# Cross-attention kernel, one core: the first batch's fifth output chunk copied by ScalarE with its bias, its residual added by an accumulating transfer of GpSimd's queue

## The chip, the core and the metric

The kernel runs on one core of a Trainium2 chip. The time is that of the device for one execution, in microseconds (us). The kernel before was run three times: 497.24, 496.01 and 496.43 us, so its median is 496.43 us. One further execution was recorded by the hardware profiler; its span, from the first to the last instruction of the program, is 494.6 us.

The engines are called as the profile calls them: PE (TensorE, matrix products; PEld is its weight load), DVE (VectorE), ACT (ScalarE), POOL (GpSimd), and SP (SyncE, which issues most transfers). Each engine works through a queue of its own in the order in which the program emits instructions; engines wait for each other through semaphores.

## What is computed

Cross-attention of 2 x 2048 tokens of width 640 (20 heads of 32) over 154 context rows of width 1024. The first 77 rows ("text") and the last 77 ("ip") have weights of their own and a softmax each; both results are added, projected, and the bias and the input itself are added. All in float32. Cut to its core:

```
q    = split(x @ Wq.T)                                  # 20 heads of 32
k, v = split(ctx[:, :77] @ Wk.T), split(ctx[:, :77] @ Wv.T)
ki, vi = split(ctx[:, 77:] @ Wk_ip.T), split(ctx[:, 77:] @ Wv_ip.T)
attend = lambda q, k, v: softmax(q @ k.T / sqrt(32)) @ v
out  = merge(attend(q, k, v) + attend(q, ki, vi))
return out @ Wo.T + bo + x
```

## The kernel before

**Layout.** Tensors lie with the channel on the partitions: 640 channels are 5 chunks of 128, and the 2048 tokens of a batch are 4 blocks of 512. A unit `u` (0 to 19) is one batch, one chunk of 4 heads and one half of the tokens; a pair of units shares a chunk (`q = u // 2`, 0 to 9; 0 to 4 are the first batch).

**Order.** The whole order is written by hand: `SCHEDULE` is a string of 1026 words, and `emit` turns each word into the instructions of one step, in that order. Since every engine has one queue, the place of a word sets its place on the queue of its engine. The words that matter here:

- `R`, `K`, `M`, `S`, `E`, `D`, `I`, `N`, `T` with `s.u` (group of 128-token rows `s` of unit `u`): scores on PE (L242), copy to the tile `pb` on ACT (L254), maxima on DVE (L290, L293), subtraction on POOL (L304), exponential on ACT (L310, or row by row with the bias at L278), sums and reciprocals on DVE (L315, L320), normalisation on POOL (L325), 32 x 32 transposes on DVE (L332). `A.q` multiplies by the values on PE (L341), `CA.q` copies the result to `aT` on ACT (L364, L368).
- `q.u.h` is a query projection on PE (L206), `cq` its copy on ACT (L220).
- The output projection of the first batch: chunks 0 to 3 of the output go through Strassen-like products `m1` to `m7` (L499, L509), whose inputs `G` POOL subtracts (L440), and which DVE adds into the tile `acc` (L524, L530). The fifth chunk (128 of the 640 output channels) has a path of its own, below.
- `V`, `X`, `F`, `Y`, `z`, `yz`: the output projection of the second batch by a fast 5 x 5 scheme, the last stage of the kernel: sums of weights (`V`, L864, L866) and of tokens (`X`, L872) on DVE and POOL, products on PE (L887), and their addition into the output on DVE (L827, L830).
- `LX`, `LQ`, `VS` and others issue transfers from SP's queue.

**The fifth chunk of the first batch**, for each token block `i` = 0 to 3: `SF.i.4` (L468, SP) loads the block's residual, 128 x 512 numbers of `x`, into the only tile `res`; `o.i@n` (L480, PE) makes the product in PSUM bank `n`; `co.i` (`store_last`, L490, DVE) adds product, bias and residual into `res`; `SS.i.4` (L474, SP) stores `res`. After the fourth block `res` is used again, for a block of the second batch (L855). The banks are 0 to 7; `R...@0` uses banks 0 to 3 and `R...@1` banks 4 to 7. `o.0` uses bank 3, `o.1` and `o.2` bank 0, `o.3` bank 7.

**Words around the fourth block.** `... E2.18 T0.18 co.3 A.8@0 N1.18 cm4.2 SS.3.4 SS.2.3 SS.2.1 G5.3 T1.18 ... V.P.0.p ... R1.19@1 CA.8 N2.18 ...`. On ACT, `E2.18` and `CA.8` follow each other; on POOL, `N1.18`, `G5.3`, `V.P.0` and `N2.18`.

Of the kernel before, what the change touches and what calls it, by code (L numbers as in the profile page):

```python
# [20 lines left out]
def kernel(  # L21
# [432 lines left out]
    def part_in(t, s, h):  # L454
        return t.rearrange("p (op s) (h t) -> p s h op t", s=2, h=2)[:, s, h]
# [6 lines left out]
    def in_dram_last(t, b, i):  # L462
        return t[ts(NC - 1, P), ds(b * S + i * TB, TB)]

    def fetch(i, part):

        if part == "last":
            nc.sync.dma_start(out=res, in_=in_dram_last(xT, 0, i))  # L468
        else:
            nc.sync.dma_start(out=part_in(acc, *part), in_=in_dram(xT, 0, i, *part))  # L470
# [17 lines left out]
    def store_last(ps, b, i):  # L488
        t = last_of(b, i)
        nc.vector.scalar_tensor_tensor(t, ps, bo_sb[:, NC - 1 :], t, ALU.add, ALU.add)  # L490
# [94 lines left out]
    for t in range(2):  # L585
# [350 lines left out]
```

## Time and profile before

| | |
|---|---|
| median of three runs (lowest to highest) | 496.43 us (496.01 to 497.24) |
| profiled execution, span | 494.6 us |
| PE busy | 489.1 us, 99% of the span |
| DVE busy | 413.9 us, 84% |
| POOL busy | 370.5 us, 75% |
| ACT busy | 309.5 us, 63% |
| granted clock of PE, mean | 1.000 |
| `co.i` on DVE (L490) | 4 instructions, 2.9 us in all, the first at 228.62 us, the last at 388.88 us |

How to read it: "busy" is the union of an engine's instructions. A row of the timeline gives start, length, engine, line, operation, the tile written and those read, the shape, how many instructions the row holds, and in brackets for how long the engine had been idle before it and what ended that idle time. Times in all views count from the start of the span.

### The profile page before, as it was taken

How to read it: one execution, taken by the hardware profiler on the slowest of the kernel's cores; microseconds unless marked ns; L12 is line 12 of the kernel's file. 1: busy time of each engine (PE TensorE's matmuls, PEld its weight loads, DVE VectorE, ACT ScalarE, POOL GpSimd, SP SyncE). 2: the span in 40 equal slices, each digit the busy share in tenths (PEclk: the TensorE clock that was granted, in tenths of full speed). 3: DMA queues.
4: the chain of work that ended last, by engine and by line, in shares of the span. 5: the costliest groups of instructions: out<-in, count | busy, mean ns of one | idle time of the engine just before them, and what ended most of it. 6: DMA issues, size and time to landing. Idle time of an engine off the chain costs nothing.

```text
span 494.6 us, 10484 instructions
## 1 busy us (share of the span) xinstructions
PE 489.1 (99%) x4116; PEld 287.7 (58%) x4116; DVE 413.9 (84%) x416; ACT 309.5 (63%) x1002; POOL 370.5 (75%) x158
## 2 busy tenths in 40 slices
PE   9999999999999999999999999999999999999997
PEld 5666648558557556456566654754755675444443
DVE  0069989989899989979988896687789898999996
ACT  1275788977687778677899786587889862100000
POOL 0069988988988988879886758475689899798700
PEclk9999999999999999999999999999999999999999
DMA  8992046203241724895540666455550212320125
GB/s 278 350 288 80 17 124 181 67 1 95 62 150 44 247 65 146 270 345 178 161 172 27 215 195 223 134 172 183 184 169 19 90 42 85 129 85 2 42 85 212
DMA packets 67105, 69.38 MB, mean 140 GB/s; under 512 B 5488, under 2 KB 47088, under 8 KB 67056
## 3 DMA queue, kind: packets, MB, share of 16 engines
q1 hardware_dynamic: 66048, 67.54, 43.7%
q10 hardware_dynamic: 1008, 1.18, 0.7%
q8 instruction: 32, 0.52, 0.4%
q14 instruction: 17, 0.14, 0.1%
HBM read 54.94 MB, written 10.49 MB: 132 GB/s over the span
## 4 chain that ended last, share of the span: by engine, by line
PE 96%; DMA 3%; ACTq 0%; ACT 0%; DVE 0%; DVEq 0%; issue 0%
PE bank L206 34%; PE bank L887 12%; PE bank L341 11%; PE bank L242 11%; PE bank L499 10%; PE bank L144 9%; PE bank L480 7%; PE bank L509 3%; DMA aT<-in_L_xattn_Wk_ip_dram 2%; DMA x<-in_x_dram 1%; ACTq L538 0%; ACT pb L254 0%; ACTq L552 0%; DVE acc L830 0%; DVEq L931 0%
## 5 line engine op out<-in xcount | busy, mean ns | idle before, releaser
L325 POOL TENSOR_TENSOR pb<-pb,rden 128x1848 f32<-128x1848 f32 (+1 forms) x60 | 176.0, 2943 | 30.4 <-DVE rden L320 23.6
L304 POOL TENSOR_TENSOR pb<-pb,mx 128x1848 f32<-128x1848 f32 (+1 forms) x39 | 121.6, 3129 | 55.4 <-DVE mx L290 55.3
L206 PE MATMUL bank<-x,wq 128*128 128x512 f32 x280 | 125.4, 598 | 0.1
L332 DVE STREAM_TRANSPOSE pb<-pb 128x1920 f32<-128x1920 f32 (+1 forms) x60 | 115.9, 1938 | 9.1 <-POOL pb L325 8.9
L290 DVE TENSOR_REDUCE mx<-pb 128x24 f32<-128x1848 f32 (+1 forms) x50 | 91.6, 1844 | 32.1 <-ACT pb L254 31.9
L254 ACT COPY pb<-bank 128x462 f32<-128x462 f32 (+1 forms) x200 | 85.3, 542 | 29.3 <-PE bank L242 28.9
L315 DVE TENSOR_REDUCE den<-pb 128x24 f32<-128x1848 f32 (+1 forms) x47 | 88.9, 1895 | 15.6 <-ACT pb L310 12.8
L206 PEld LDWEIGHTS bank<-x,wq 128*128 128x128 f32 x280 | 51.7, 190 | 60.0 <-issue 58.8
L310 ACT ACTIVATE pb<-pb 128x1848 f32<-128x1848 f32 (+1 forms) x39 | 65.6, 1684 | 17.5 <-POOL pb L304 17.4
L278 ACT ACTIVATE pb<-bank,mx 128x77 f32<-128x77 f32 x208 | 60.4, 387 | 6.5 <-DVE mx L293 6.5
L278 ACT ACTIVATE pb<-pb,mx 128x77 f32<-128x77 f32 x184 | 54.1, 356 | 1.9 <-DVE mx L290 1.8
L341 PE MATMUL bank<-pb,v 32*32 32x512 f32 x1600 | 55.2, 597 | 0.0
L206 PE MATMUL bank<-x,aT 128*128 128x512 f32 x116 | 51.8, 596 | 0.0
L242 PEld LDWEIGHTS bank<-kT,qT 32*128 32x128 f32 x1024 | 36.1, 184 | 21.6 <-issue 13.3
L144 PE MATMUL bank<-wo_ct,aT 128*128 128x154 f32 x320 | 46.0, 297 | 0.7 <-DMA aT<-in_L_xattn_Wk_ip_dram 0.4
L144 PEld LDWEIGHTS bank<-wo_ct,aT 128*128 128x128 f32 x320 | 43.0, 188 | 4.7 <-issue 3.0
L242 PE MATMUL bank<-kT,qT 32*128 32x154 f32 x1024 | 45.1, 305 | 0.0
L278 ACT ACTIVATION_READ_ACCUMULATOR pb<-bank,mx 128x1 f32 x168 | 44.0, 266 | 0.0
L341 PEld LDWEIGHTS bank<-pb,v 32*32 32x32 f32 x1600 | 29.0, 103 | 22.7 <-issue 10.1
L480 PE MATMUL bank<-aT,wo_ct 128*128 128x512 f32 x80 | 36.3, 595 | 0.0
L206 PEld LDWEIGHTS bank<-x,aT 128*128 128x128 f32 x116 | 21.4, 190 | 23.7 <-issue 23.5
L220 ACT ACTIVATE qT<-bank 128x512 f32<-128x512 f32 x32 | 19.3, 631 | 23.4 <-PE bank L206 23.4
(83 smaller groups left out, 524.2 us busy)
## 6 DMA issues: line engine op xcount, KB each, us to landing
x<-in_x_dram SPq DMA_DIRECT2D x20, 1280.0 KB, 6.7
out_dram<-acc SPq DMA_DIRECT2D x19, 256.0 KB, 2.9
x<-in_x_dram SPq DMA_DIRECT2D x17, 256.0 KB, 5.9
acc<-in_x_dram SPq DMA_DIRECT2D x16, 256.0 KB, 4.4
out_dram<-x SPq DMA_DIRECT2D x15, 256.0 KB, 2.0
v<-vS SPq DMA_DIRECT2D x160, 20.0 KB, 2.7
aT<-in_L_xattn_Wk_dram SPq DMA_DIRECT2D x5, 512.0 KB, 6.0
aT<-in_L_xattn_Wk_ip_dram SPq DMA_DIRECT2D x5, 512.0 KB, 5.5
```

The source lines that it names most:

```text
L144: nc.tensor.matmul(keys_in(out), loaded[n][:, k, :], cT[:, k, :, t, :], start=(k == 0), stop=(k == NCC - 1))
L206: nc.tensor.matmul(pq, weight_of(q)[:, k, :], xs[place_of(u, h)][:, k, :], start=(k == 0), stop=(k == NC - 1), skip_group_check=loose,)
L242: nc.tensor.matmul(ps[g][:, ts(t, 2 * L)], qTs[(u, h)][g * D : (g + 1) * D, ts(st, P)], kT[g * D : (g + 1) * D, c, b].rearrange("p t l -> ...
L254: nc.scalar.copy(keys_of(u, s)[:, :, g], ps[g][:, : n * 2 * L].rearrange("p (n l) -> p n l", n=n))
L278: nc.scalar.activation(row, row if ps is None else rows_in(ps[g], n)[:, t, x], AF.Exp, bias=maxs[(u, s)][:, *one], accum_out=None if den i ...
L290: nc.vector.tensor_reduce(mx, rows_of(u, s), AX.X, ALU.max, negate=negate)
L304: nc.gpsimd.tensor_tensor(rows_of(u, s), rows_of(u, s), maxs[(u, s)].unsqueeze(3).to_broadcast([P, n, 2, L]), ALU.subtract)
L315: nc.vector.tensor_reduce(den_of(u, s), rows_of(u, s), AX.X, ALU.add)
L325: nc.gpsimd.tensor_tensor(rows_of(u, s), rows_of(u, s), rdens[(u, s)].unsqueeze(3).to_broadcast([P, n, 2, L]), ALU.mult)
L332: nc.vector.transpose(p, p)
L341: nc.tensor.matmul(pa[r][g * D : (g + 1) * D, :], v4s[q % 2][rows, g, k, :], zones[rows, :, g, k, :], start=(k == 0), stop=(k == NK - 1),)
L480: nc.tensor.matmul(ps, wo[:, k, ts(NC - 1, P)], rows_of_attention(b, k)[:, i], start=(k == 0), stop=(k == NC - 1),)
```

## The change

`co.i` moves from DVE to ACT: one activation (identity with the bias) copies the product from PSUM to `res`. The load of the residual, `SF.i.4`, is left out. A new word, `AX.i`, takes its place: a transfer issued from GpSimd's queue which reads the residual from memory and adds it into `res` (`accum_op=ALU.add`). `SS.i.4` stores `res` as before; it now follows `AX.i`.

```diff
     def fetch(i, part):
-        if part == "last":
-            nc.sync.dma_start(out=res, in_=in_dram_last(xT, 0, i))
-        else:
-            nc.sync.dma_start(out=part_in(acc, *part), in_=in_dram(xT, 0, i, *part))
+        nc.sync.dma_start(out=part_in(acc, *part), in_=in_dram(xT, 0, i, *part))
...
     def store_last(ps, b, i):
-        t = last_of(b, i)
-        nc.vector.scalar_tensor_tensor(t, ps, bo_sb[:, NC - 1 :], t, ALU.add, ALU.add)
+        nc.scalar.activation(last_of(b, i), ps, AF.Identity, bias=bo_sb[:, NC - 1 :])
+
+    def add_residual(i):
+        nc.gpsimd.dma_start(out=last_of(0, i), in_=in_dram_last(xT, 0, i), accum_op=ALU.add)
...
+        elif k == "AX":
+            add_residual(x)
```

In `SCHEDULE` the four words `SF.i.4` go, four words `AX.i` come, and the four `SS.i.4` move a little later; `co.i` keeps its place. All other words stand in the order in which they stood. With a few neighbours:

```
before: ... I1.10 K2.11 D0.11 N1.10 R1.12@0 M2.11 ...        after: ... N1.10 AX.0 R1.12@0 M2.11 ...
before: ... G7.1 T2.13 E1.13 ...                             after: ... G7.1 T2.13 AX.1 E1.13 ...
before: ... G5.2 cm5.1 R0.15@1 co.2 LX.17.0 m3.1 K0.15 SS.2.4 cm3.1 ...
after:  ... G5.2 cm5.1 R0.15@1 co.2 LX.17.0 m3.1 K0.15 AX.2 cm3.1 ...
before: ... co.3 A.8@0 N1.18 cm4.2 SS.3.4 SS.2.3 ...         after: ... co.3 A.8@0 N1.18 cm4.2 AX.3 SS.2.3 ...
```

POOL's queue around the fourth block, before. L325 is the normalisation (`N0.18`, `N1.18`, then `N2.18`), L440 `G5.3`, L866 a sum of weights.

```order
L325 TENSOR_TENSOR pb<-pb,rden_0_3385 128x12x154
L325 TENSOR_TENSOR pb<-pb,rden_1_3401 128x12x154
L440 TENSOR_TENSOR x_85<-aT 128x512
L866 TENSOR_TENSOR pb<-wo_ct 128x128
L325 TENSOR_TENSOR pb<-pb,rden_2_3515 128x8x154
L440 TENSOR_TENSOR aT<-aT 128x2x256
```

The same place after the change.

```order
L325 TENSOR_TENSOR pb<-pb,rden_0_3384 128x12x154
L325 TENSOR_TENSOR pb<-pb,rden_1_3400 128x12x154
L489 DMA res<-in_x_dram 128x512
L440 TENSOR_TENSOR x_85<-aT 128x512
L866 TENSOR_TENSOR pb<-wo_ct 128x128
L325 TENSOR_TENSOR pb<-pb,rden_2_3514 128x8x154
```

The transfer `AX.3` (L489) stands on POOL between `N1.18` and `G5.3`; it waits for a semaphore of ACT.

ACT's queue at the same place after the change. L278 is `E2.18`, row by row; L364 is `CA.8`; L254 is the copy of scores `K1.19`.

```order
L220 ACTIVATE qT_0_3396<-bank_72 128x512
L278 ACTIVATE pb,den_2_3402<-pb,mx_2_3398 128x77 x16
L486 ACTIVATE res<-bank_74,bo_sb 128x512
L364 COPY aT<-bank_67 128x4x4x32
L364 COPY aT<-bank_68 128x4x4x32
L364 COPY aT<-bank_69 128x4x4x32
L364 COPY aT<-bank_70 128x4x4x32
L254 COPY pb<-bank_71 128x3x154
```

`co.3` (L486) stands behind the 16 exponentials of `E2.18` and ahead of `CA.8`. Before, no instruction stood between these two, and `co.3` was on DVE behind the transposes of `T0.18`.

POOL's queue around the first block after the change. L410 sums weights, L325 is `N1.10` and then `N0.11`, L304 `S1.11`.

```order
L410 TENSOR_TENSOR wo_ct<-wo_ct 128x2x2x128
L325 TENSOR_TENSOR pb<-pb,rden_1_2056 128x12x154
L489 DMA res<-in_x_dram 128x512
L325 TENSOR_TENSOR pb<-pb,rden_0_2089 128x12x154
L304 TENSOR_TENSOR pb<-pb,mx_1_2118 128x12x154
```

`AX.0` stands between `N1.10` and `N0.11`, which followed each other before.

115 rows, old and new, of the table SCHEDULE are left out of this document.

## Prediction

> **What bounds the kernel now.** I read the page first: busy shares and the chain that ended last.
>
> ```profile
> PE 489.1 (99%) x4116; PEld 287.7 (58%) x4116; DVE 413.9 (84%) x416; ACT 309.5 (63%) x1002; POOL 370.5 (75%) x158
> PE 96%; DMA 3%; ACTq 0%; ACT 0%; DVE 0%; DVEq 0%; issue 0%
> ```
>
> PE is busy for 99% of the span and is 96% of the chain; the 3% of transfers lie before the first large products. An average can hide stages, so I cut the span into windows (length, then busy us of each engine).
>
> ```profile
> 17.00:95.00 78.00, 78.00 (x700) 50.09 (x701) 63.90 (x49) 55.24 (x120) 61.88 (x21) 1.00 0.56 155
> 95.00:190.00 95.00, 95.00 (x1076) 59.15 (x1074) 88.23 (x69) 72.09 (x176) 82.41 (x29) 1.00 0.31 90
> 190.00:285.00 95.00, 94.88 (x811) 54.50 (x806) 85.03 (x85) 78.47 (x303) 79.93 (x34) 1.00 0.60 196
> 285.00:380.00 95.00, 95.00 (x840) 55.87 (x839) 75.42 (x77) 73.61 (x287) 66.33 (x26) 1.00 0.52 164
> 380.00:437.00 57.00, 57.00 (x526) 34.53 (x525) 51.59 (x65) 27.30 (x117) 51.38 (x30) 1.00 0.23 75
> ```
>
> From 17 to 437 us PE idles 0.12 us (95.00 - 94.88), at a granted clock of 1.00. The change takes no product away, so by this view there is next to nothing to win: what DVE is spared can only shorten waits of PE, and there are hardly any. Ends of products are modelled, so short waits may hide in the busy time. I bound the gain at 0.6 us, an estimate of five times the visible idle time. What is left to read is whether the change makes PE wait.
>
> **The change part by part.** What goes and what comes:
>
> ```profile
> L490 DVE SCALAR_TENSOR_TENSOR res<-bank,bo_sb,res x4: 706/724/743, 228.6 to 388.9; 128x512 f32<-128x512 f32 x4
> L220 ACT ACTIVATE qT<-bank 128x512 f32<-128x512 f32 x32 | 19.3, 631 | 23.4 <-PE bank L206 23.4
> L440 POOL TENSOR_TENSOR aT<-aT 128x512 f32<-128x512 f32 x8 | 10.2, 1272 | 0.4 <-PE bank L499 0.3
> L468 SPq DMA_DIRECT2D res<-in_x_dram x4: 462/528/890, 195.5 to 325.2; - x4
> ```
>
> (min/median/max ns in the first and last row; busy us and mean ns in the others.) DVE is rid of 4 x 0.724 = 2.9 us. ACT gains four copies; the nearest row is its scaled copy of a 128x512 bank, 0.631 us, so 4 x 0.63 = 2.5 us. SP loses four issues of 0.53 us (median). POOL gains four issues of a transfer, each with a wait for ACT.
>
> The length **d** of such an issue on POOL is shown nowhere, since POOL issues nothing before. From below: SP's issue of the same load, at least 0.46 us. From above: POOL's longest operation, 3.29 us (rows below). I take 1.27 us, POOL's pass over the same 128x512 shape, because it is the row of the same engine and size. Below nothing is excluded: an instruction is added and none leaves POOL.
>
> Now the four places. `co.i` and `AX.i` cost nothing where ACT is idle when the product is ready, and POOL idle where the issue stands.
>
> ```profile
> 229.54 2.85 ACT L254 COPY pb<-bank 128x462 f32<-128x462 f32 x7 [1.66 <-PE bank L242]
> 235.28 3.29 POOL L325 TENSOR_TENSOR pb<-pb,rden 128x1848 f32<-128x1848 f32 x1 [0.23 <-DVE rden L320]
> 239.38 3.29 POOL L304 TENSOR_TENSOR pb<-pb,mx 128x1848 f32<-128x1848 f32 x1 [0.80 <-DVE mx L290]
> 251.92 0.36 ACT L278 ACTIVATION_READ_ACCUMULATOR pb<-bank,mx 128x1 f32 x1
> 252.57 0.81 PE L242 MATMUL bank<-kT,qT 32*128 32x154 f32 x16
> 282.60 3.55 ACT L278 ACTIVATE pb<-bank,mx 128x77 f32<-128x77 f32 x16 [1.45 <-DVE mx L293]
> 288.05 2.25 POOL L325 TENSOR_TENSOR pb<-pb,rden 128x1232 f32<-128x1232 f32 x1 [2.71 <-DVE rden L320]
> 311.07 1.89 ACT L254 COPY pb<-bank 128x462 f32<-128x462 f32 x4 [3.81 <-PE bank L242]
> 318.44 3.29 POOL L304 TENSOR_TENSOR pb<-pb,mx 128x1848 f32<-128x1848 f32 x1 [7.26 <-DVE mx L290]
> ```
>
> Blocks 1 and 2 (`co.1`, `co.2`, `AX.1`, `AX.2`) fall into ACT's idle 1.45 and 3.81 us and into POOL's idle 2.71 and 7.26 us: 0. At block 0 `co.0` falls into ACT's 1.66 us. `AX.0` stands ahead of the row at 235.28; behind it are 0.23 and 0.80 us of idle time, so 1.27 - 1.03 = 0.24 us of lateness is left on POOL at 239.38. That goes on to ACT's exponentials, whose last ends at 252.28 (251.92 + 0.36); PE, which wants the banks that they free, comes at 252.57. The 0.29 us between them cover it: 0. Without that cover it would cost the 0.24 us.
>
> Block 3 is different. `co.3` stands behind the 16 exponentials `E2.18`, and POOL's queue stops at `AX.3` until `co.3` is done.
>
> ```profile
> 391.91 0.34 ACT L278 ACTIVATE pb<-pb,mx 128x77 f32<-128x77 f32 x1
> 392.37 2.05 ACT L364 COPY aT<-bank 128x512 f32<-128x512 f32 x4
> 386.95 3.29 POOL L325 TENSOR_TENSOR pb<-pb,rden 128x1848 f32<-128x1848 f32 x1 [0.21 <-DVE rden L320]
> 390.19 1.29 POOL L440 TENSOR_TENSOR x<-aT 128x512 f32<-128x512 f32 x1
> 391.65 0.46 POOL L866 TENSOR_TENSOR pb<-wo_ct 128x128 f32<-128x128 f32 x1 [0.17 <-PE bank L341]
> 392.87 2.25 POOL L325 TENSOR_TENSOR pb<-pb,rden 128x1232 f32<-128x1232 f32 x1 [0.76 <-DVE rden L320]
> 395.15 1.51 DVE L332 STREAM_TRANSPOSE pb<-pb 128x1280 f32<-128x1280 f32 x1 [2.36 <-POOL pb L325]
> 397.93 1.27 POOL L440 TENSOR_TENSOR aT<-aT 128x512 f32<-128x512 f32 x1 [0.34 <-PE bank L499]
> 408.94 8.79 POOL L325 TENSOR_TENSOR pb<-pb,rden 128x1848 f32<-128x1848 f32 x3
> 417.77 2.18 DVE L332 STREAM_TRANSPOSE pb<-pb 128x1920 f32<-128x1920 f32 x1 [0.36 <-POOL pb L325]
> 427.41 1.48 DVE L872 TENSOR_TENSOR pb<-aT 128x1024 f32<-128x1024 f32 x1 [0.36 <-PE bank L341]
> 438.71 1.41 DVE L827 SCALAR_TENSOR_TENSOR x<-x,bo_sb,bank 128x512 f32<-128x512 f32 x2 [0.20 <-PE bank L887]
> 439.37 1.93 PE L887 MATMUL bank<-pb,wo_ct 128*128 128x512 f32 x4
> ```
>
> Step by step:
> - The last exponential is the row at 391.91, and `CA.8` follows at 392.37. `co.3` takes that place and ends at 392.37 + 0.63 = 393.00. DVE did it at 388.88; `E2.18` does not move.
> - POOL reaches `AX.3` at 390.24 (386.95 + 3.29) and waits 2.76 us. Then comes the issue: `G5.3` (row 390.19) starts at 393.00 + 1.27 = 394.27, so it is **4.08 us late**.
> - Behind it POOL idles 0.17 and 0.76 us today: 3.15 us late at `N2.18` (392.87). The transposes at 395.15 already wait for it today, so DVE is late by the same.
> - One more idle time of 0.34 us: 2.81 us late at 397.93. From there POOL has no idle gap until 417.73 (408.94 + 8.79), so 2.81 us reach DVE at 417.77, which today waits for just this.
> - DVE then works almost without a gap to 440.12 (438.71 + 1.41). Its idle 0.36 and 0.20 us wait for PE, which is late itself by then, so they absorb between 0 and 0.56 us: 2.25 to 2.81 us late.
> - PE's second product in the row at 439.37 starts half a row later, at some 440.2, and takes what DVE left at 440.12: at most 0.1 us of cover. So PE loses 2.15 to 2.81 us, and I take the middle, 2.5 less a little for the hidden gain: **+2.4 us**.
>
> In general the loss is d + 0.9 to d + 1.5 us: with 0.46 us 1.3 to 2.0, with 3.29 us 4.2 to 4.8. Two smaller things at this place: `CA.8` comes 0.63 us later on ACT, and bank 7, which `co.3` frees, is free at 393.0 and not at 389.6, so the scores `R1.19` may make PE wait some tenths. Both run beside the larger delay and are not added to it.
>
> On SP the stores wait for the landing of `AX.i`. The load of `res` issued by SP landed within 3.5 to 9.2 us, and I take the same for the new transfer. `SS.3.4` is followed on SP by stores that nothing here waits for until `res` is loaded again after 420 us. So SP costs 0.
>
> Sum: the profiled execution would go from 494.6 to 497.0 us. The median of the runs lies 1.8 us above that span (496.43 - 494.6), and I leave that as it is: **498.8 us**.
>
> One rule speaks against POOL as the issuer. The Trainium skill (SBUF — State Buffer, "SBUF: two separate sides") says that GpSimd cannot write the descriptors of its transfers while DVE holds the port pair that both share. At `AX.3` it would change nothing by this trace: DVE idles from 392.79 to 395.15 (row 395.15, 2.36 us).
>
> **The rivals.**
>
> *The issue is dearer than a pass (17%).* It could be held up behind a DVE operation, or the first one could pay for being the first. Place: `AX.0`, with DVE at work around it. Price: one transposition more, 2.18 us (row 417.77), so 3.45 us; less 1.03 us of idle time and the 0.29 us before PE, PE loses 2.1 us there, and the later 2.4 us stay: 500.9 us. For it: POOL has never issued anything before. Against it: POOL's own passes over `pb` take 3.29 us in every row here, with DVE at work beside most of them. The Trainium skill (GPSIMD Engine Reference, "Instruction dispatch") gives some 6 us for the first call of freshly loaded code; by that the kernel would come out beyond this price. No run here shows such a load.
>
> *POOL doesn't stop at the wait (16%).* If the wait of `AX.3` is held beside the queue, and `G5.3` and `N2.18` go past it, the 2.76 us fall away. Then d alone is left, and 1.27 us meets 0.17 + 0.76 + 0.34 = 1.27 us of idle time: no loss, 496.4 us. It decides as soon as `G5.3` can start before 393.0. For it: `G5.3` and `N2.18` don't touch `res`. Against it: POOL's other waits hold everything behind them, as in the row at 318.44 (7.26 us).
>
> *DVE was the hidden bound (4%).* If the 2.9 us of DVE shorten waits that the modelled ends hide, and POOL catches up, the kernel gains more than I allow, say half of the 2.9: 495.0 us. Against it: 0.12 us of idle time in 420 us.
>
> **How the numbers follow.** Forecast 63%, rivals 17, 16 and 4%. About 0.3%, 1.5 us, is what a measurement of this kernel can tell from no change. In the forecast the loss exceeds 1.5 us unless d is below some 0.3 us (or the sum is too high by 0.9): I give that one case in eight. Slower: 0.63 x 7/8 + 0.17 = 0.72. Same: 0.63/8 + 0.16 = 0.24. Faster: 0.04. The range reaches down to no change, 496.3, which leaves out the gain and half of the second rival (12%), and up to 501.3, which holds the first rival's price and leaves out what is dearer (8%). The forecast's own range, from d = 0.46 to 2.5 us, is 497.7 to 500.4.
>
> **What would show it.** Right: on POOL before `G5.3` an idle time of some 2.8 us ended by ACT, an issue of 1 to 1.5 us, the transposes after `N2.18` about 3 us late against 395.15, POOL without a gap to about 420, and PE late by over 2 us from 440 us to the end; blocks 0 to 2 show no shift of PE above 0.3 us. Wrong: `G5.3` starting before 393 us, an issue row far from 1.27 us, or PE late before 390 us. If `co.3` ran ahead of `E2.18` on ACT, the place would be misread altogether.

## The result and the profile after

| | before | after |
|---|---|---|
| median of 4 runs each, on one chip | 496.53 us (496.01 to 497.24) | 498.26 us (497.65 to 498.39) |
| profiled execution, span | 494.6 us | 496.6 us |

The ratio is 1.0042, with a 95% interval of 1.0028 to 1.0055: the change makes the kernel slower, by 1.7 us of the median and 2.0 us of the profiled span.

First the page of the changed kernel: its busy times and the chain that ended last.

```profile
PE 489.9 (99%) x4116; PEld 287.6 (58%) x4116; DVE 411.7 (83%) x412; ACT 311.9 (63%) x1006; POOL 373.9 (75%) x162
...
PE 88%; DVE 5%; DMA 3%; ACT 2%; POOL 1%; issue 1%; SPq 0%; ACTq 0%; DVEq 0%
```

DVE is relieved of 2.2 us (413.9 to 411.7) and ACT gains 2.4. PE still looks busy for 99% of the span, so the page's first part hides the loss. The chain gives it away: PE had 96% of it, and now DVE, ACT and POOL hold 8%. The windows of the change, cut as those of before (length, then busy us of PE, PEld, DVE, ACT and POOL), say where:

```profile
17.00:95.00 78.00, 78.00 (x701) 50.09 (x702) 64.07 (x49) 55.43 (x120) 62.05 (x21) 1.00 0.56 154
95.00:190.00 95.00, 95.00 (x1076) 59.00 (x1074) 88.25 (x69) 72.15 (x177) 82.40 (x29) 1.00 0.31 89
190.00:285.00 95.00, 94.77 (x806) 54.46 (x803) 83.95 (x83) 79.75 (x306) 80.92 (x35) 1.00 0.62 194
285.00:380.00 95.00, 95.00 (x840) 55.94 (x839) 74.73 (x76) 74.35 (x289) 67.91 (x28) 1.00 0.52 164
380.00:437.00 57.00, 56.17 (x523) 34.13 (x522) 49.13 (x62) 27.43 (x117) 50.09 (x31) 1.00 0.27 80
```

Up to 380 us PE stands as before (0.23 us of idle time against 0.12). In the last window it now idles 0.83 us, and the granted clock is 1.00 throughout. A narrower cut puts all of that into ten microseconds; of before,

```profile
400.00:410.00 10.00, 10.00 (x53) 7.23 (x52) 8.84 (x16) 8.44 (x37) 10.00 (x6) 1.00 0.01 2
```

and of the change:

```profile
400.00:410.00 10.00, 9.17 (x50) 6.69 (x50) 9.97 (x15) 6.35 (x27) 9.92 (x5) 1.00 0.08 28
```

The chain of waits between 385 and 412 us names what is behind it (start, length, what; only the longer pieces are listed). Before, it is PE alone:

```profile
387.23 5.48 PE bank L341 x151
393.70 2.79 PE bank L499 x12
399.21 1.06 PE bank L499 x4
402.74 2.79 PE bank L499 x12
407.25 3.43 PE bank L480 x8
```

In the change it leaves PE and comes back at 405.66:

```profile
386.57 3.60 ACT pb L278 x21
390.27 1.90 ACT pb L278 x11
393.92 1.31 POOL x L440
395.63 2.21 POOL pb L325
398.01 1.29 issue
399.30 2.03 DVE mx L290
402.76 2.07 DVE mx L290
405.66 1.13 PE bank L498 x4
408.52 3.43 PE bank L477 x8
```

ACT's exponentials `E2.18`, then POOL's `G5.3` (L440) and `N2.18` (L325), then DVE, then PE. The links in the timeline of the change, engine by engine:

```profile
391.73 0.34 ACT L278 ACTIVATE pb<-pb,mx 128x77 f32<-128x77 f32 x1
...
392.07 0.67 ACT L486 ACTIVATE res<-bank,bo_sb 128x512 f32<-128x512 f32 x1
...
386.76 3.29 POOL L325 TENSOR_TENSOR pb<-pb,rden 128x1848 f32<-128x1848 f32 x1 [0.21 <-DVE rden L320]
393.03 0.88 POOL L489 DMA_DIRECT2D res<-in_x_dram  x1 [2.98 <-ACT res L486]
393.64 1.58 POOL L440 TENSOR_TENSOR x<-aT 128x512 f32<-128x512 f32 x1
...
395.30 2.53 POOL L325 TENSOR_TENSOR pb<-pb,rden 128x1232 f32<-128x1232 f32 x1
...
397.86 1.51 DVE L332 STREAM_TRANSPOSE pb<-pb 128x1280 f32<-128x1280 f32 x1 [5.26 <-POOL pb L325]
...
405.66 1.13 PE L498 MATMUL bank<-aT,x 128*128 128x256 f32 x4 [0.71 <-DVE acc L523]
...
420.09 2.18 DVE L332 STREAM_TRANSPOSE pb<-pb 128x1920 f32<-128x1920 f32 x1 [0.56 <-POOL pb L325]
...
491.71 1.03 PE L887 MATMUL bank<-pb,wo_ct 128*128 128x256 f32 x4
```

`co.3` (L486) follows the last exponential; POOL is free at 390.05 (386.76 + 3.29), stands still for 2.98 us at `AX.3` (L489), and the transposes on DVE wait 5.26 us where they waited 2.36. The last products start at 491.71; in the trace of before that row reads:

```profile
490.07 1.03 PE L887 MATMUL bank<-pb,wo_ct 128*128 128x256 f32 x4
```

**A scale for all that follows.** I paired every PE product and POOL operation of a trace with the same one of before, in order, and took differences. Profiled executions differ by up to 1.3 us at the start, where the first loads land (14 to 17 us). So each run has a base, the median difference of PE's products between 320 and 391 us, which is taken off; for the change it is -0.18 us. Two numbers come out: how late `G5.3` ends on POOL, and how late PE is at its last products. In the change `G5.3` ends at 393.64 + 1.58 = 395.22 against 390.19 + 1.29 = 391.48, so 3.74 + 0.18 = 3.92 us late; PE is 491.71 - 490.07 + 0.18 = 1.82 us late. Of these 1.82 us, 0.32 are there at 393.6 us, 1.45 by 405 and 1.50 by 422, and the rest comes at 439 to 441. Behind the last products both traces run alike up to the issue of the last store; from there to the end of the span the change takes 0.4 us longer, which with PE's 1.64 us makes the span's 2.0. The base also takes off what PE loses ahead of 320 us. In the change that is nothing: from 17 to 391 us the median difference of every stretch lies within 0.05 us of -0.18. Experiment 1 is the exception, told there.

### The profile page after: what moved, and what is told of

It reads as the page before. It is cut to its first block, busy times and chain, and to the rows that moved or that the text cites. A ratio compares the mean times of both kernels' runs of the same rounds, so it can differ in the third digit from the quotient of the medians.

```text
span 496.6 us, 10484 instructions
## 1 busy us (share of the span) xinstructions
PE 489.9 (99%) x4116; PEld 287.6 (58%) x4116; DVE 411.7 (83%) x412; ACT 311.9 (63%) x1006; POOL 373.9 (75%) x162
## 4 chain that ended last, share of the span: by engine, by line
PE 88%; DVE 5%; DMA 3%; ACT 2%; POOL 1%; issue 1%; SPq 0%; ACTq 0%; DVEq 0%
PE bank L206 32%; PE bank L887 12%; PE bank L341 10%; PE bank L242 9%; PE bank L144 9%; PE bank L498 8%; PE bank L477 6%; PE bank L508 2%; DMA aT<-in_L_xattn_Wk_ip_dram 2%; DVE mx L290 2%; DVE den L315 1%; ACT pb L278 1%; DMA aT<-in_L_xattn_Wq_dram 1%; DVE pb L332 1%; ACT pb L254 1%
## 5 line engine op out<-in xcount | busy, mean ns | idle before, releaser
L325 POOL TENSOR_TENSOR pb<-pb,rden 128x1848 f32<-128x1848 f32 (+1 forms) x60 | 176.5, 2952 | 28.4 <-DVE rden L320 22.2
L304 POOL TENSOR_TENSOR pb<-pb,mx 128x1848 f32<-128x1848 f32 (+1 forms) x39 | 121.5, 3128 | 53.9 <-DVE mx L290 53.7
L254 ACT COPY pb<-bank 128x462 f32<-128x462 f32 (+1 forms) x200 | 85.3, 538 | 24.6 <-PE bank L242 24.2
L278 ACT ACTIVATE pb<-bank,mx 128x77 f32<-128x77 f32 x208 | 60.6, 388 | 5.8 <-DVE mx L293 5.8
L278 ACT ACTIVATE pb<-pb,mx 128x77 f32<-128x77 f32 x184 | 54.1, 358 | 1.9 <-DVE mx L290 1.8
L278 ACT ACTIVATION_READ_ACCUMULATOR pb<-bank,mx 128x1 f32 x168 | 44.0, 267 | 0.0
```

Of the source, the lines that this page charges most:

```text
L254: nc.scalar.copy(keys_of(u, s)[:, :, g], ps[g][:, : n * 2 * L].rearrange("p (n l) -> p n l", n=n))
L278: nc.scalar.activation(row, row if ps is None else rows_in(ps[g], n)[:, t, x], AF.Exp, bias=maxs[(u, s)][:, *one], accum_out=None if den i ...
L304: nc.gpsimd.tensor_tensor(rows_of(u, s), rows_of(u, s), maxs[(u, s)].unsqueeze(3).to_broadcast([P, n, 2, L]), ALU.subtract)
L325: nc.gpsimd.tensor_tensor(rows_of(u, s), rows_of(u, s), rdens[(u, s)].unsqueeze(3).to_broadcast([P, n, 2, L]), ALU.mult)
```

## The experiments

Theory **A**: POOL stands still at `AX.3` until ACT has done `co.3`, and what stands behind it in POOL's queue is late through DVE to PE; the issue adds its own length. **B**: the four issues on POOL cost, wherever they stand. **C**: `co.3` on ACT, ahead of `CA.8`, costs by itself. **D**: the accumulating transfers disturb others. Where a median alone does not tell theories apart, the traces do. Each group was timed against the kernel before on the same chip: 495.92 us for the first four runs, 495.81 for the next four, 495.71 for the last two.

**1. The transfer later in POOL's queue.** `AX.3` stands behind `N2.18`, not ahead of `G5.3`:

```diff
-... cm4.2 AX.3 SS.2.3 SS.2.1 G5.3 ... R1.19@1 CA.8 N2.18 m1.3@0 ...
+... cm4.2 SS.2.3 SS.2.1 G5.3 ... R1.19@1 CA.8 N2.18 AX.3 m1.3@0 ...
```

> AX.3 is put behind N2.18 on POOL's queue; nothing else moves. Theory A (POOL stands still at AX.3 until ACT has done co.3): POOL reaches AX.3 at about 395.1, after co.3 has ended (392.7), so there is no wait; what is left is one issue of 0.9 us, of which 0.3 us of idle time takes a part: PE loses 0 to 0.4 us, so 496.3 to 497.0 us. Theory B (the four issues on POOL cost the time, wherever they stand), theory C (co.3 on ACT ahead of CA.8 costs it, through later copies and the later bank 7) and theory D (the accumulating transfers disturb other transfers): unchanged against the changed kernel, about +1.7 us, 498.2 us.

Measured: 496.68 us, ratio 1.0013 (1.0004 to 1.0022). POOL in this run:

```profile
389.78 1.28 POOL L440 TENSOR_TENSOR x<-aT 128x512 f32<-128x512 f32 x1
...
392.44 2.25 POOL L325 TENSOR_TENSOR pb<-pb,rden 128x1232 f32<-128x1232 f32 x1 [0.75 <-DVE rden L320]
394.63 0.88 POOL L489 DMA_DIRECT2D res<-in_x_dram  x1
```

The same transfer with the same issue of 0.88 us, moved past two operations, no longer waits, and `G5.3` and `N2.18` are on time. Against its base PE loses 0.30 us, all at 393.6 us, and nothing later. That is C, and it is small. Ahead of the stretch on which the base is taken, PE loses another 0.46 us in this trace, at a wait for a load of `x` (0.23 us show as idle time) that PE has in no other trace:

```profile
295.16 4.56 PE L206 MATMUL bank<-x,wq 128*128 128x512 f32 x10 [0.23 <-DMA x<-in_x_dram]
```

SP issues this load (1280 KB) at 285 to 287 us. In the four traces without `AX.1` (before, 4, 5, 9) it lands 6.5 us after its issue, 2.5 us ahead of the product that needs it. In the eight with `AX.1`, which POOL issues 1.3 us earlier, it takes 8.1 to 9.4 us: 8.4 in the change, which leaves PE 0.6 us, and 9.4 in this run, which leaves it none.

**2. The copy earlier in ACT's queue.** `co.3` stands ahead of `E2.18`, `AX.3` where the change has it:

```diff
-... E2.18 T0.18 co.3 A.8@0 ...
+... co.3 E2.18 T0.18 A.8@0 ...
```

> co.3 is put ahead of E2.18 on ACT, where ACT idles 1.46 us and the product of o.3 is ready; AX.3 stays. Theory A: co.3 ends near 386 us, POOL does not wait at AX.3, and its issue of 0.9 us meets 0.93 us of idle time behind it: 0, so 496.2 to 496.8 us. Theory C: co.3 no longer stands ahead of CA.8 and bank 7 is free early: the same. Theories B and D: unchanged, +1.7 us, 498.2 us.

Measured: 496.24 us, ratio 1.0007 (0.9999 to 1.0016). The copy now falls into ACT's idle time before the exponentials, and POOL goes straight through:

```profile
389.72 0.87 POOL L489 DMA_DIRECT2D res<-in_x_dram  x1
390.33 1.58 POOL L440 TENSOR_TENSOR x<-aT 128x512 f32<-128x512 f32 x1
...
392.71 2.25 POOL L325 TENSOR_TENSOR pb<-pb,rden 128x1232 f32<-128x1232 f32 x1 [0.40 <-DVE rden L320]
```

PE loses 0.00 us against its base: the 0.30 us of experiment 1 are gone as well. All four issues and all four accumulating transfers are still there, so B and D fall as causes of the change's loss. (The load of experiment 1 shows that the transfers do disturb one other; here it still lands 0.5 us early enough.)

**3. The copy on DVE.** ACT is left alone; DVE adds product and bias, and the four transfers stay:

```diff
-        nc.scalar.activation(last_of(b, i), ps, AF.Identity, bias=bo_sb[:, NC - 1 :])
+        nc.vector.tensor_scalar(last_of(b, i), ps, bo_sb[:, NC - 1 :], None, ALU.add)
```

> The copy with the bias is done by DVE again (all four blocks), the residual still comes by AX.i from POOL, all words in the places of the changed kernel. Theory A: DVE ends co.3 near 389.6, before POOL reaches AX.3 (390.05), so no wait: 0 to +0.3 us, 496.4 to 496.8 us. Theory C: 0 as well. Theories B and D: +1.7 us, 498.2 us.

Measured: 496.36 us, ratio 1.0008 (0.9999 to 1.0017); PE loses nothing against its base. With the copy on DVE or off it (experiment 2), the time is the same: DVE's relief is worth nothing that can be measured.

**4. No transfer.** The copies stay on ACT as in the change, the four words `AX.i` go (the fourth is shown):

```diff
-... cm4.2 AX.3 SS.2.3 ...
+... cm4.2 SS.2.3 ...
```

> The copy with the bias on ACT as in the changed kernel, but no AX.i: the first batch's fifth output chunk lacks its residual. Theories A, B and D: no wait, no issue and no transfer on POOL, so only DVE's relief of 2.9 us and ACT's load are left: -0.5 to +0.2 us, 496.0 to 496.7 us. Theory C: co.3 still stands ahead of CA.8: +1.7 us, 498.2 us.

Measured: 496.39 us, ratio 1.0008 (0.9999 to 1.0017). PE loses 0.31 us, again all at 393.6 us, as in experiment 1. So C is worth 0.3 us in the trace, with `AX.3` absent or merely late.

**5. The fourth block alone.** Blocks 0 to 2 keep load, product and DVE's addition of before; only block 3 has ACT's copy and the transfer:

```diff
+        if i == 3:
+            nc.scalar.activation(t, ps, AF.Identity, bias=bo_sb[:, NC - 1 :])
+        else:
+            nc.vector.scalar_tensor_tensor(t, ps, bo_sb[:, NC - 1 :], t, ALU.add, ALU.add)
```

> Only the fourth block is changed: the first three keep load, product and DVE's addition as before. Theory A (POOL stands still at AX.3, and that reaches PE's end): the whole loss stays, 1.4 to 2.0 us over the kernel before, the same as the full change; POOL idles some 3 us ahead of the transfer and PE is 1 to 1.6 us late from 440 us on. Theory B (each issue on POOL costs) and D (each accumulating transfer costs): a quarter of the loss, some 0.4 us.

Measured: 498.39 us, ratio 1.0053 (1.0041 to 1.0066), 2.6 us over before; that is above the stated 2.0, and PE's loss in the trace, 1.97 us, above the stated 1.6. `G5.3` is 4.06 us late. Block 3 alone makes the whole loss; the other three issues add nothing to it. (The interval of the ratio meets that of the change, so the higher median isn't shown to be more than noise.) The issue is the run's only one and took 1.00 us where the change's fourth took 0.88:

```profile
393.19 1.00 POOL L496 DMA_DIRECT2D res<-in_x_dram  x1 [2.99 <-ACT res L491]
393.93 1.57 POOL L440 TENSOR_TENSOR x<-aT 128x512 f32<-128x512 f32 x1
```

**6. Two issues without the wait.** Experiment 2 with `AX.3` cut into two halves of 128x256:

```diff
-            nc.gpsimd.dma_start(out=last_of(0, i), in_=in_dram_last(xT, 0, i), accum_op=ALU.add)
+        for cols in SIDES if i == 3 else (slice(0, TB),):
+            nc.gpsimd.dma_start(
+                out=last_of(0, i)[:, cols], in_=in_dram_last(xT, 0, i)[:, cols], accum_op=ALU.add
+            )
```

> The version without the wait (bias copy of the fourth block ahead of E2.18 on ACT), and its transfer AX.3 cut into two half transfers of 128x256, the second issued behind the first. This measures the price of an issue when POOL doesn't wait. Theory A: an issue alone is a small matter; POOL has 0.17 + 0.76 us of idle time behind it and 0.34 us later, two issues are 1.7 us at most, so 0 to 0.5 us over the version with one issue. Theory B (the issue itself is what costs): one issue more costs POOL another 0.9 us that nothing covers, and PE loses 0.8 us or more.

Measured: 496.31 us, ratio 1.0006 (0.9998 to 1.0015), where experiment 2 had 1.0007. `G5.3` ends 1.76 us late where one issue made it 0.88, so an issue costs POOL 0.88 us; PE loses 0.00 us. Two issues fit into the slack, the lateness that the engines' idle times absorb on the way to PE.

**7. A plain transfer.** The full change without the addition in the transfer:

```diff
-        nc.gpsimd.dma_start(out=last_of(0, i), in_=in_dram_last(xT, 0, i), accum_op=ALU.add)
+        nc.gpsimd.dma_start(out=last_of(0, i), in_=in_dram_last(xT, 0, i))
```

> The full change with a plain transfer instead of the accumulating one: the residual overwrites the sum of product and bias in res, so the fifth chunk of the first batch holds only the residual. Everything else, the wait of AX.3 for co.3 too, is as in the change. Theory A: as slow as the change, 1.4 to 2.0 us over the kernel before. Theory D (reading, adding and writing back of the accumulating transfers disturb others): most of the loss goes, under 0.6 us over the kernel before.

Measured: 498.10 us, ratio 1.0043 (1.0029 to 1.0057), 2.3 us over before, which is above the stated 2.0. It is as slow as the change, so the adding isn't the cause, and D falls once more. The issue is shorter:

```profile
393.09 0.58 POOL L489 DMA_DIRECT2D res<-in_x_dram  x1 [2.97 <-ACT res L486]
393.69 1.29 POOL L440 TENSOR_TENSOR x<-aT 128x512 f32<-128x512 f32 x1
```

`G5.3` is 3.61 us late and PE loses 1.52: 0.31 less of the one, 0.30 less of the other.

**8. The wait alone.** At `AX.3` POOL makes an addition of 128x1 on `res` in place of the issue:

```diff
+        if i == 3:
+            t = last_of(0, i)[:, :1]
+            nc.gpsimd.tensor_tensor(t, t, t, ALU.add)
+        else:
+            nc.gpsimd.dma_start(out=last_of(0, i), in_=in_dram_last(xT, 0, i), accum_op=ALU.add)
```

> The full change, but at AX.3 POOL issues no transfer: a small addition of 128x1 on POOL stands there, which reads and writes res and so waits for co.3 in the same way. The fourth block's fifth chunk lacks the residual, and its first column is doubled. Theory A: the wait of about 2.9 us stays and the issue (0.87 us) shrinks to some 0.1 to 0.3 us, so of the change's loss some 0.6 us goes: 0.8 to 1.4 us over the kernel before. If the issue were what counts (B): under 0.5 us over the kernel before.

Measured: 497.03 us, ratio 1.0028 (1.0018 to 1.0038), 1.2 us over before.

```profile
391.68 0.66 ACT L486 ACTIVATE res<-bank,bo_sb 128x512 f32<-128x512 f32 x1
...
392.42 0.20 POOL L491 TENSOR_TENSOR res<-res 128x1 f32<-128x1 f32 x1 [2.75 <-ACT res L486]
392.57 1.27 POOL L440 TENSOR_TENSOR x<-aT 128x512 f32<-128x512 f32 x1
```

`G5.3` is 2.93 us late, PE loses 0.86 us. The wait without a transfer behind it keeps about half of PE's loss.

**9. The order of the stores.** All versions without the stall stay 0.3 to 0.8 us over before. What they share is the order of SP's stores, and that SP issues no `SF.i.4`; this run tries the first alone. It is the kernel before with its four `SS.i.4` at the places of the change (the loads set behind them are `SF.2.4` and `SF.3.4`, where the expectation names `SF.1.4` and `SF.2.4`); the third block is shown:

```diff
-... K0.15 SS.2.4 cm3.1 ... q.16.1@1 SF.3.4 D0.15 I0.15 ...
+... K0.15 cm3.1 ... q.16.1@1 D0.15 SS.2.4 SF.3.4 I0.15 ...
```

> The kernel before with only the four stores SS.i.4 at the later places on SP that they have in the change (and the loads SF.1.4 and SF.2.4 behind them where they would overtake). All versions without the stall of POOL were 0.3 to 0.8 us over the kernel before, though their traces show no later PE. If the order on SP, which they all share, is the cause: 0.3 to 0.5 us over the kernel before. If it is not: under 0.2 us.

Measured: 495.96 us, ratio 1.0003 (0.9994 to 1.0011), PE's loss 0.00. The median lies 0.25 us over before, just above the bound of "not the cause", and the interval holds none as well as 0.5 us. It is inconclusive: where the rest of these versions comes from stays open.

**10. The wait and two issues.** The full change with the edit of experiment 6, to test the rule that runs 1 to 8 suggest where it had not been used:

> The full change, with AX.3 cut into two half transfers of 128x256: the wait of POOL for co.3 as in the change, and one issue more behind it. Theory A: what comes late at G5.3 beyond some 2.1 us of slack is lost one for one, so the second issue, 0.9 us, which cost nothing without the wait, costs PE 0.7 to 1.0 us more than the change here: 2.4 to 3.4 us over the kernel before. If the loss of the change were bounded by something else (PE's products catching up, or the wait alone): no more than the change, 1.4 to 2.0 us over the kernel before.

Measured: 498.56 us, ratio 1.0067 (1.0054 to 1.0081), 2.85 us over before. POOL and PE:

```profile
392.33 1.77 POOL L490 DMA_DIRECT2D res<-in_x_dram  x2 [2.97 <-ACT res L486]
393.48 1.93 POOL L440 TENSOR_TENSOR x<-aT 128x512 f32<-128x512 f32 x1
...
403.17 1.97 PE L501 MATMUL bank<-aT,x 128*128 128x256 f32 x8 [1.00 <-DVE acc L532]
405.85 1.13 PE L501 MATMUL bank<-aT,x 128*128 128x256 f32 x4 [0.72 <-DVE acc L526]
```

The second issue, which cost nothing in experiment 6, costs PE 0.87 us here (2.69 against 1.82), and a second wait for DVE's additions into `acc` appears ahead of the first.

**All runs on one scale** (us; lateness and loss against each run's base, from the traces; the last column from the medians):

| run | `G5.3` ends late | PE late at the end | difference | median over before |
|---|---|---|---|---|
| 1, 4, 9 | 0.0 | 0.30, 0.31, 0.00 | | 0.76, 0.47, 0.25 |
| 2, 3 | 0.88 | 0.00 | | 0.32, 0.44 |
| 6 | 1.76 | 0.00 | | 0.50 |
| 8 | 2.93 | 0.86 | 2.07 | 1.22 |
| 7 | 3.61 | 1.52 | 2.09 | 2.29 |
| the change | 3.92 | 1.82 | 2.10 | 1.73 |
| 5 | 4.06 | 1.97 | 2.09 | 2.58 |
| 10 | 4.79 | 2.69 | 2.10 | 2.85 |

PE's loss is the lateness of `G5.3` less 2.1 us, one for one, and nothing below that, but for the 0.3 us of `co.3` in runs 1 and 4 (and the 0.46 us of run 1 ahead of its base). Theory A holds. None of the versions is faster than the kernel before.

## Why the prediction was right

The forecast (slower, by a stall of POOL at `AX.3`) was right in mechanism and sign: 498.8 us against 498.26, +2.4 against +1.7 us. By its own steps:

- **No gain to be had: right.** Experiments 2 and 3 differ in DVE's work and not in their time.
- **Blocks 0 to 2 cost nothing: right, with a price overlooked.** Experiment 5 has none of their edits and loses no less. But the prediction asked only whether ACT and POOL were idle there, not what the transfer of block 1 does to a load beside it: that takes some 2 of the 2.5 us of slack that PE has at 295 us, and in the trace of experiment 1 it costs 0.46 us of time. The 0.24 us that block 0 left on POOL did not come: the first issue took 1.01 us and the subtractions behind it were not late.
- **`co.3` behind `E2.18`, end at 393.00: right.** It ended at 392.74, or 392.92 with the base put back.
- **POOL waits 2.76 us: right.** The row has 2.98. The difference is a pause that the prediction had at nothing: the transfer starts 0.29 us after `co.3` ends (392.74 to 393.03).
- **The issue d = 1.27 us: too long.** It takes 0.88 us (experiment 6). That pause and shorter issue nearly cancel is luck: `G5.3` ends 3.92 us late where the sum had 4.08.
- **Two idle times of POOL absorb 0.93, a third 0.34 us: right.** `N2.18` ends 2.89 us late (3.92 less 1.03; predicted 3.15), and DVE's row at 420.09 is 2.50 us late (predicted 2.81).
- **The mis-sized term is what is absorbed between there and PE.** The prediction let DVE and PE absorb "between 0 and 0.56 us" and at most 0.1 more, and took the middle. It was 2.50 less 1.82, 0.68 us: all of it. In all, 2.1 us of lateness vanish on the way from `G5.3` to PE, where the sum had 1.3 to 1.9, and 1.7 as taken.
- **The place of the loss: wrong in part.** The prediction followed POOL to 420 us and DVE to 440, and had PE lose everything there. Most of it, 1.13 us of 1.82, is lost between 393.6 and 405: the late transposes make DVE's additions into `acc` (L523) late, and PE's products wait for these at 405.66. The prediction had not looked at what DVE does for PE between 395 and 417 us. Only 0.32 us come at 439 to 441. Still it is this later place that sets the total. In the five runs with the stall PE is late at 405 by the lateness of `G5.3` less 2.46 us (1.45 in the change, 0.48 in experiment 8, 2.33 in experiment 10), and at the end by the same less 2.10. And DVE has no idle time there that PE could have caused: the row that waited 0.36 us for PE before (427.41) waits for nothing in the change, and DVE's lateness reaches PE:

```profile
429.05 1.22 DVE L872 TENSOR_TENSOR pb<-aT 128x1024 f32<-128x1024 f32 x1
...
440.80 2.14 PE L887 MATMUL bank<-pb,wo_ct 128*128 128x512 f32 x4
```

- **`co.3` ahead of `CA.8`, "some tenths, not added": right as far as seen.** It is 0.3 us where it stands alone (experiments 1 and 4). That it runs beside the larger delay is argued, not tried, since every run with the stall has it too: PE waits 0.71 us for DVE at 405.66, and without the 0.3 us it would only have come there earlier and waited longer. In the change PE's 24 scores `R1.19` stretch from 1.07 to 1.39 us; whether they wait for bank 7, which `co.3` frees, or for something behind `CA.8` was not tried apart.
- **SP costs 0: right in the trace of the change.** The additions landed 4.2 to 7.4 us after their issue, within the 3.5 to 9.2 assumed, and no store behind them held PE. The load of `x` that SP issues at 286 us was late, as said above, but not too late.

The rivals. *The issue is dearer than a pass*: no, 0.86 to 1.01 us each. Of being held up behind DVE nothing is seen: the first issue of the change ran beside a transposition that began 0.11 us after it, and the second began in the middle of one,

```profile
234.52 1.01 POOL L489 DMA_DIRECT2D res<-in_x_dram  x1
234.63 2.18 DVE L332 STREAM_TRANSPOSE pb<-pb 128x1920 f32<-128x1920 f32 x1 [0.36 <-POOL pb L325]
...
283.92 1.51 DVE L332 STREAM_TRANSPOSE pb<-pb 128x1280 f32<-128x1280 f32 x1 [0.42 <-POOL pb L325]
...
285.07 0.86 POOL L489 DMA_DIRECT2D res<-in_x_dram  x1
```

The second took no longer than the others (0.86 us), and the first no longer than the only one of experiment 5 (1.00 us), beside which DVE was idle. What these two of 1.0 us share is that they are the first of their run, and that price is 0.13 us (1.01 against 0.88), not a transposition's 2.18. The Trainium skill (GPSIMD Engine Reference, "Instruction dispatch") has some 6 us for the first call of freshly loaded code; no such pause stands at the first issue here. *POOL doesn't stop at the wait*: no, 2.98 us of idle time, and experiment 8 loses by a wait alone. *DVE was the hidden bound*: no, as above.

What stays open: medians lie above the loss in the table by 0.2 to 0.8 us in all runs but the change. The trace of one execution says nothing about a median at that size, and experiment 9 did not settle it. In run 1 the excess, 0.46 us, is just what PE lost at 295 us in its trace. Other executions with `AX.1` may wait there too, but runs 4, 5 and 9, without `AX.1`, have an excess as well (0.16, 0.61 and 0.25 us).

## What to carry to other kernels

A transfer that must wait for another engine is not free on a compute engine's queue: the wait holds everything behind it, here for 2.98 us, while the issue itself is 0.88 us. Before such a word is placed, compare the time at which its queue arrives with the time at which its operand is ready. Then take the lateness through every engine in the order in which they wait for each other, and look at every place at which the bounding engine waits for one of them: here 2.46 us of slack lay ahead of the first, 2.10 us ahead of the last, and the smallest slack decides whether the stall costs nothing and how much of it is paid. And ask what the transfer takes from the loads beside it, not only what its issue takes from its queue.

## What the runs showed of the hardware

- **An accumulating issue on POOL takes as long at half the size; a plain one is shorter.** Accumulating: 0.88 us for 128x512 (experiment 1), and 1.77 us for two of 128x256 (experiment 10). Plain, 128x512: 0.58 us (experiment 7).
- **The first issue of a run is 0.13 us longer.** 1.01 against 0.88 us in the change, 0.71 against 0.58 us with plain transfers (experiment 7), and 1.00 us for the only one of experiment 5.
- **A transfer starts later after a wait than an addition.** 0.29 us after the end of `co.3` for the transfer of the change, 0.08 us for the addition of experiment 8 (391.68 + 0.66 = 392.34 to 392.42).
- **Rows on POOL behind an accumulating issue read too long.** `G5.3` has 1.58 us behind one such issue and 1.93 behind two, with a start inside the issue's row; behind a plain issue it has 1.29, as before. The operations follow each other at the old pitch, so ends are to be compared, not starts.
- **A transfer from POOL's queue delays a load from SP's.** The load of `x` that SP issues 1.3 us behind `AX.1` lands 8.1 to 9.4 us after its issue in eight traces, against 6.5 us in the four without `AX.1`. It does so with a plain transfer as well (8.1 us, experiment 7).
